# An attention and mixture-of-experts block: the maxima of two score parts in one bank, taken in one instruction

## The chip, the cores and the metric

The kernel runs on one core of a Trainium2 chip. The metric is the device time of one execution in microseconds (us). Before the change the median of three runs is 1061.35 us (1058.91 to 1062.14). The five engines of the core run side by side: PE multiplies matrices (its weight loads are shown as PEld), DVE works on vectors, ACT applies functions, POOL does general work and issues some transfers, SP issues most transfers. PE writes its products into PSUM, which has eight banks; DVE and ACT read them there.

## The reference

The input is four batches of 1024 tokens with 256 features. Layer norm with a modulation, causal attention with 16 heads of 16 features, an output projection with a gate, a second layer norm, a router that picks two of eight experts for each token, the experts (256 to 512 to 256) and a gated sum:

```python
scores = jnp.einsum('bhqd,bhkd->bhqk', Q, K) / np.sqrt(D_HEAD)
causal = jnp.triu(jnp.full((t, t), -jnp.inf, dtype=scores.dtype), k=1)
attn = jax.nn.softmax(scores + causal, axis=-1)
O = jnp.einsum('bhqk,bhkd->bhqd', attn, V)
```

The softmax needs, for each query and head, the maximum of the scores over the keys that are not later than the query. Everything is in float32.

## The kernel before

Attention works in **units**: a unit is four heads of one batch (NQD = 4 units for each of 4 batches, 16 in all, numbered u from 0 to 15). The four heads of a unit stand in the four groups of 32 partitions of `qTs[u % 3]` and `kTs[u % 3]`, so PE multiplies for four heads side by side, each in 32 of its 128 rows. Each unit needs two things. First the **maxima** of the scores, with queries in partitions and keys along the free axis: `m_parts` (line 829) fills a bank `ps_max` of 128 x 512 for one head, and `maxima` (lines 849 and 851) takes the largest of each row on DVE. These maxima are turned by PE (`max_rows`, line 861), copied by ACT and sent by SP into a spare row of `qTs`, so that they are subtracted when, second, the **scores** are multiplied again with keys in partitions: `s_parts` (line 896) fills a bank `ps_s`, `weigh` (line 913) adds the causal mask by a small bf16 product of `qmask` and `unit` (the identity), `exponential` (line 921) runs on ACT into `pt`, and `av_step` (line 940) multiplies `pt` with the values.

Both are cut into nine **steps**, so that each bank of 512 columns is full. Step i of the maxima takes the parts of `m_steps[i]`, each of them (tile of 128 queries, half of the keys, first column). Tiles 0 to 3 are the first half of the queries, tiles 4 to 7 the second; the second half needs all of the first 512 keys as well (`mf`, no mask) and then its own half (`mx`, masked in its last 128 columns). Three steps have two parts in one bank: step 1 (tile 2 with 384 columns and tile 0 with 128), step 2 (tiles 1 and 5, 256 each) and step 8 (tile 6 with 384, tile 4 with 128). The others have one part of 512.

`maxima` treats each part by itself. Where there is no mask (`mf`) it is one plain reduction (line 849). Where there is one it is a custom instruction (line 851) that adds the mask `cmask` and reduces, starting from the maximum of the unmasked half where there is one; a second, short instruction then reads the accumulator out into `mx`. So a bank with two parts takes four instructions.

`both` runs step i of the scores of unit u together with step i of the maxima of unit u + 1, in two half steps. A half step fills two score banks and two maxima banks, their matmuls in turn, then the maxima go to DVE, then the masks and exponentials of the scores; after the first half the av matmuls of the step before follow. In the first half the masks are written in four pieces of 32 columns of the array (`w = HW`), as the av matmuls that follow are; in the second half in one piece. Pool `ps_sc` has seven banks, used in turn by these four and by the small products between the steps (`ps_mi`: projections of the next batch, layer norm turns, routing of the batch before); the eighth holds `av`. A bank is free again when ACT or DVE has read it, and PE, which executes in order, waits for that. So do the other engines wait in order: what stands behind a waiting instruction waits as well.

In the main loop units 0 to 14 run `both` for all nine steps (unit 0 begins a little differently: its own maxima are taken by `m_alone`, which lets PE add the masks, lines 878 and 849), and unit 15 has scores alone. Between the steps the loop issues pieces of other work: layer norm (L67 makes the normalized rows that PE turns in line 76), projections (773, 748), the output projection (1003), the router of the batch before (240 to 331, on DVE above all, from unit 7 on), gates. A scheduler orders the instructions of each engine by its own estimates, so that the order around the steps is near the program's but not the same. Attention ends at about 753 us; then the experts run in blocks of 256 tokens (lines 550 to 567).

## Time and profile before

| | |
|---|---|
| median of three runs | 1061.35 us (1058.91 to 1062.14) |
| the profiled execution's own time | 1067.35 us |
| its span, first to last instruction | 1065.6 us |
| mean granted PE clock (1 is full speed) | 0.971 |
| instructions | 22453 |
| stretch of units 4 to 14 | 232.28 to 724.38 us: PE busy 485.67 of 492.10, DVE 385.70, ACT 265.38, clock 0.98 |
| unit 15 and the end of attention | 724.38 to 753.00 us |
| experts | 753.00 to 1065.60 us: PE busy 284.24 of 312.60 |

Busy time is the time in which an engine has an instruction under way. For PE this is not the same as useful work: matmuls overlap and their ends are modelled, so a matmul can seem busy while the next one waits. What tells is the time from the start of one piece of work to the start of the next, the idle time and what ended it, and the clock that the chip granted PE in the stretch. In the profile's groups the parts of a line are: line, engine, operation, names (out <- in) and shapes, count, busy us and mean ns of one, and the idle time of the engine just before them with what ended it.

### The profile page before, as it was taken

Reading aid. Unit: us, or ns where it says so; the run is one execution under the profiler, and the core shown is the slowest. Engines: PE = TensorE matmul, PEld = TensorE weight load, DVE = VectorE, ACT = ScalarE, POOL = GpSimd, SP = SyncE. Lnnn points to the kernel's source line nnn. Section 1 sums busy time; section 2 is a strip of 40 time slices with the busy share of each in tenths; the row PEclk is TensorE's granted clock in tenths of the full one; section 3 lists DMA queues with packets and bytes.
Section 4 is the critical chain, followed back from the end, with each engine's and each line's share of the span. In section 5 each row is a group of like instructions: output and inputs, shape, how many; then the busy total and the mean of one; then the engine's idle time right before and its main releaser. Section 6 shows DMA issues by size and latency. Waiting matters only on the chain. (4 is left out here: it accounts for less than half of the span.)

```text
span 1065.6 us, 22453 instructions
## 1 busy us (share of the span) xinstructions
PE 1009.5 (95%) x8154; PEld 597.5 (56%) x8154; DVE 750.8 (70%) x2349; ACT 509.7 (48%) x963; POOL 239.5 (22%) x231
## 2 busy tenths in 40 slices
PE   5899999999999999999999999998689999999994
PEld 4554534544544544454463444533368888888893
DVE  4787867766787877788868788782466686566761
ACT  4125654655555555655545546446313264444540
POOL 4000010000000001222001330015131764444344
PEclk9899999999999999999999999999889999999997
DMA  8310120110111202123010331002489956443432
GB/s 272 82 31 8 38 47 14 35 39 14 38 46 49 56 24 48 45 65 86 19 42 28 78 83 36 22 28 72 135 260 289 314 105 158 72 66 65 66 62 25
DMA packets 68686, 81.58 MB, mean 77 GB/s; under 512 B 19480, under 2 KB 50072, under 8 KB 68448
## 3 DMA queue, kind: packets, MB, share of 16 engines
q1 hardware_dynamic: 55008, 63.26, 21.7%
q0 software_dynamic: 13296, 16.89, 8.9%
q8 instruction: 64, 1.05, 0.4%
q14 instruction: 46, 0.38, 0.1%
q10 hardware_dynamic: 272, 0.00, 0.0%
HBM read 45.11 MB, written 24.93 MB: 66 GB/s over the span
## 5 line engine op out<-in xcount | busy, mean ns | idle before, releaser
L921 ACT ACTIVATE pt<-ps_s 128x512 f32<-128x512 f32 x576 | 313.0, 596 | 295.0 <-PE ps_s L913 183.2
L829 PE MATMUL ps_max<-kT,qT 32*128 32x512 f32 (+3 forms) x1536 | 376.6, 531 | 4.6 <-DVE mf L849 2.9
L896 PE MATMUL ps_s<-qT,kT 32*128 32x512 f32 (+3 forms) x1536 | 343.9, 527 | 4.2 <-DMA qT<-rows 2.4
L896 PEld LDWEIGHTS ps_s<-qT,kT 32*128 32x128 f32 x1536 | 134.5, 186 | 143.3 <-issue 44.9
L849 DVE TENSOR_REDUCE mf<-ps_max 128x1 f32<-128x512 f32 x256 | 164.0, 682 | 60.4 <-PE ps_max L829 55.2
L851 DVE CUSTOM_DVE_ANT_0 unused<-ps_max,cmask,mf 128x256 f32<-128x256 f32 (+3 forms) x256 | 140.5, 549 | 46.9 <-PE ps_max L829 27.1
L829 PEld LDWEIGHTS ps_max<-kT,qT 32*128 32x128 f32 x1536 | 153.4, 188 | 34.3 <-DVE mx L851 11.0
L940 PE MATMUL av<-pt,vaug 128*32 128x512 f32 (+3 forms) x1536 | 160.3, 505 | 0.8 <-ACT ot L948 0.8
L972 POOL TENSOR_TENSOR oc<-oc,rec 64x512 f32<-64x512 f32 x32 | 40.6, 1270 | 506.9 <-DMA rec<-inv 453.8
L567 POOL DMA_INDIRECT out_dram<-y,xb x67 | 107.8, 1609 | 131.1 <-DVE gs L529 55.7
L851 DVE CUSTOM_DVE_ANT_0 unused<-ps_max,cmask 128x128 f32<-128x128 f32 (+2 forms) x232 | 114.3, 493 | 29.5 <-PE ps_max L829 15.1
L550 PE MATMUL ps_h<-xt,wa 128*128 128x256 f32 (+1 forms) x608 | 125.2, 358 | 1.3 <-DVE xt L538 1.3
L561 PE MATMUL ps_y<-wb,hs 128*128 128x256 f32 x536 | 122.7, 379 | 0.0
L550 PEld LDWEIGHTS ps_h<-xt,wa 128*128 128x128 f32 x608 | 103.6, 193 | 12.3 <-DVE xt L538 1.6
L561 PEld LDWEIGHTS ps_y<-wb,hs 128*128 128x128 f32 x536 | 100.6, 190 | 13.2 <-ACT hs L554 0.2
L529 DVE SCALAR_TENSOR_TENSOR gs<-x,share,gs 128x256 f32<-128x256 f32 x201 | 85.2, 477 | 1.0
L554 ACT ACTIVATE hs<-ps_h 128x512 f32<-128x512 f32 x67 | 39.8, 597 | 86.4 <-PE ps_h L550 76.9
L940 PEld LDWEIGHTS av<-pt,vaug 128*32 128x32 f32 x1536 | 38.1, 112 | 76.4 <-issue 67.4
L343 POOL DMA_INDIRECT slots<-hr,sloti x64 | 63.7, 995 | 76.5 <-ACT sloti L342 55.5
L566 DVE TENSOR_TENSOR y<-ps_y,gs 128x256 f32<-128x256 f32 x67 | 25.9, 419 | 72.2 <-PE ps_y L561 69.6
L913 PEld LDWEIGHTS <-qmask 128*32 128x32 bf16 (+1 forms) x1328 | 30.2, 97 | 66.6 <-issue 59.1
L913 PE MATMUL ps_s<-unit,qmask 128*32 128x128 bf16 (+1 forms) x1328 | 57.5, 227 | 0.1
(220 smaller groups left out, 924.2 us busy)
## 6 DMA issues: line engine op xcount, KB each, us to landing
w_s<-in_w_dram SPq DMA_DIRECT2D x16, 512.0 KB
xb<-slots SPq DMA_DIRECT2D x29, 259.0 KB
qT<-qc SPq DMA_DIRECT2D x64, 64.0 KB
kT<-kc SPq DMA_DIRECT2D x64, 64.0 KB
oc<-ot SPq DMA_DIRECT2D x128, 32.0 KB
rec<-inv SPq DMA_DIRECT2D x32, 128.0 KB
out_dram<-x SPq DMA_DIRECT2D x8, 512.0 KB
wa<-in_w_dram SPq DMA_DIRECT2D x8, 512.0 KB
```

The costliest lines, as they stand in the source:

```text
L343: sent = nc.gpsimd.indirect_dma_start(out=slots, out_offset=bass.IndirectOffsetOnAxis(ap=at, axis=0), in_=hr[:, t, :], in_offset=None,).ins
L529: nc.vector.scalar_tensor_tensor(gs[:, j, :], gb[:, b, :], share[:, j, b : b + 1], gs[:, j, :], ALU.mult, ALU.add)
L550: nc.tensor.matmul(ps[:, k, :], w[:, dc, fc * P : (fc + 1) * P], xt[:, dc, :], start=(dc == 0), stop=(dc == NDC - 1),)
L561: nc.tensor.matmul(ps[:, j, :], hs[:, fc, j * P : (j + 1) * P], w[:, fc, :], start=(fc == 0), stop=(fc == NFC - 1),)
L567: added = nc.gpsimd.indirect_dma_start(out=out_rows, out_offset=bass.IndirectOffsetOnAxis(ap=xb[:, j, D : D + 1].bitcast(I32), axis=0), in ...
L829: nc.tensor.matmul(ps[:, at : at + n], qTs[u % 3][r : r + HW, qt * P : (qt + 1) * P], kTs[u % 3][r : r + HW, kb * 512 : kb * 512 + n], sta ...
L849: nc.vector.tensor_reduce(top, ps[:, at : at + n], AX.X, ALU.max)
L851: nc.vector.tensor_tensor_reduce(out=unused[:, 0:n], in0=ps[:, at : at + n], in1=cmask[:, 512 - n : 512], scale=1.0, scalar=st["mf", u][:, ...
L896: nc.tensor.matmul(ps[:, at : at + n], kTs[u % 3][r : r + HW, kt * P : (kt + 1) * P], qTs[u % 3][r : r + HW, (qb + 1) * 512 - n : (qb + 1) ...
L913: nc.tensor.matmul(ps[k : k + w, at : at + P], qmask[:, k : k + w], unit, start=False, stop=at == masked[-1],)
L921: nc.scalar.activation(pt[:, 0:n], ps[:, 0:n], AF.Exp)
L940: nc.tensor.matmul(av[HW * j : HW * (j + 1), 512 - n : 512], vaug[b % 2][:, kt, 4 * qd + j, :], pts[j][:, at : at + n], start=(kt == 0), s ...
```

## The change

For the maxima of units 5 to 15, in the three steps with two parts, PE adds the masks to `ps_max` as it does for the scores, and one plain reduction of the whole bank takes all maxima by pieces: in step 2 two pieces of 256 columns (the maxima of tiles 1 and 5), in steps 1 and 8 four pieces of 128 columns, of which three belong to one tile and the fourth to the other. The pieces go to a small tile `mp`; `join`, five small DVE operations in a unit, puts them together after steps 2 and 8, with the maxima of the unmasked half where there are any. For these units the parts of steps 0 and 3 are exchanged: tile 3 (masked) comes in step 0 and the unmasked part of tile 5 in step 3. For the maxima of units 0 to 4 nothing changes.

```diff
+        m_joint = [m_steps[3], *m_steps[1:3], m_steps[0], *m_steps[4:]]
+
+        def joint(u):
+            return u > NQD
+
+        def m_list(u):
+            return m_joint if joint(u) else m_steps
...
+        def tops_of(u):
+            if ("mx", u, 0) not in st:
+                both_halves = mxp.tile([P, 2, 4, 4], F32, tag="mx2", name="mx2")
+                for half in range(2):
+                    st["mx", u, half] = both_halves[:, half]
+                    st["mp", u, half] = mxp.tile([P, 4, 4], F32, tag=f"mp{half}", name="mp")
+                st["mx2", u] = both_halves
+
+        def joint_maxima(u, i, j, ps):
+
+            tops_of(u)
+            if m_size(*m_joint[i][0][:2]) == 256:
+                out, n = st["mx2", u][:, :, j, 1], 256
+            else:
+                out, n = st["mp", u, m_joint[i][0][0] // 4][:, j, :], P
+            nc.vector.tensor_reduce(out, ps.rearrange("p (a n) -> p a n", n=n), AX.X, ALU.max)
+
+        def join(u, half):
+
+            mx, mp = st["mx", u, half], st.pop(("mp", u, half))
+            nc.vector.tensor_reduce(mx[:, :, 2], mp[:, :, 0:3], AX.X, ALU.max)
+            if half == 0:
+                nc.vector.tensor_copy(mx[:, :, 0], mp[:, :, 3])
+            else:
+                mf = st["mf", u]
+                nc.vector.tensor_tensor(mx[:, :, 0], mp[:, :, 3], mf[:, :, 0], ALU.max)
+                nc.vector.tensor_tensor(mx[:, :, 1:3], mx[:, :, 1:3], mf[:, :, 1:3], ALU.max)
...
         def both(u, i, u_max, i_max):
 
             pts = []
+            two = joint(u_max) and len(m_joint[i_max]) > 1
             for h in range(2):
                 scores, tops, parts = [], [], []
                 for j in (2 * h, 2 * h + 1):
-                    for of, banks in ((s_parts(u, i, j), scores), (m_parts(u_max, i_max, (j + 2) % 4), tops)):
+                    for of, banks in ((s_parts(u, i, j), scores), (m_parts(u_max, i_max, (j + 2) % 4, two), tops)):
...
                 in_turn(*parts)
+                if two:
+                    w = P if h else HW
+                    for ps in tops:
+                        for part in m_joint[i_max]:
+                            at = part[2] + m_size(*part[:2]) - P
+                            for k in range(0, P, w):
+                                nc.tensor.matmul(
+                                    ps[k : k + w, at : at + P], unit[:, k : k + w], qmask,
+                                    start=False, stop=part == m_joint[i_max][-1],
+                                )
                 for k in range(2):
-                    maxima(u_max, i_max, (2 * h + k + 2) % 4, tops[k])
+                    (joint_maxima if two else maxima)(u_max, i_max, (2 * h + k + 2) % 4, tops[k])
                 pts.extend(weigh(i, scores, h == 0))
...
+            if joint(u_max) and i_max in (2, 8):
+                join(u_max, i_max // 8)
```

`m_parts` and `maxima` take their parts from `m_list(u)` instead of `m_steps`. The step i of unit u carries the maxima of unit u + 1, so the new instructions stand in steps 1, 2 and 8 of units 4 to 14.

More of the change, by code (lines that the diff above doesn't have):

```diff
@@ L826, in fill @@
             def fill(k):
-                qt, kb, at = m_steps[i][k]
+                qt, kb, at = m_list(u)[i][k]
                 n = m_size(qt, kb)
@@ L831, in fill @@
                     kTs[u % 3][r : r + HW, kb * 512 : kb * 512 + n],
-                    start=(k == 0), stop=(k == len(m_steps[i]) - 1 and not open_end),
+                    start=(k == 0), stop=(k == len(m_list(u)[i]) - 1 and not open_end),
                 )
-            return ps, [lambda k=k: fill(k) for k in range(len(m_steps[i]))]
+            return ps, [lambda k=k: fill(k) for k in range(len(m_list(u)[i]))]
         def maxima(u, i, j, ps, masked=()):
-            for part in sorted(m_steps[i], key=lambda part: (part in masked, part[2]), reverse=True):
+            for part in sorted(m_list(u)[i], key=lambda part: (part in masked, part[2]), reverse=True):
                 qt, kb, at = part
@@ L844, in maxima @@
                 kind = ("mx", u, half) if kb == half else ("mf", u)
+                if joint(u) and kind[0] == "mx":
+                    tops_of(u)
                 if kind not in st:
@@ L855, in maxima @@
                     )
+        def tops_of(u):
[6 more added lines that the diff above has]
+        def joint_maxima(u, i, j, ps):
+            tops_of(u)
+            if m_size(*m_joint[i][0][:2]) == 256:
[12 more added lines that the diff above has]
+                nc.vector.tensor_tensor(mx[:, :, 1:3], mx[:, :, 1:3], mf[:, :, 1:3], ALU.max)
         def max_rows(u, half):
```

## The prediction

> **What bounds the kernel now.** I read the page's busy shares first, then the loop of score steps (232 to 724 us holds all changed work) by windows, then one clean step in order of time, then the groups by shape for the prices.
>
> ```profile
> PE 1009.5 (95%) x8154; PEld 597.5 (56%) x8154; DVE 750.8 (70%) x2349; ACT 509.7 (48%) x963; POOL 239.5 (22%) x231
> ```
>
> PE is busy nearly all the time, but matmuls are pipelined, so the share does not say whether PE works or waits with one in flight. The windows do. Columns: stretch, length, busy time (instructions) of PE, PEld, DVE, ACT, POOL, granted clock, DMA.
>
> ```profile
> 282.99:297.29 14.30, 14.30 (x169) 8.33 (x168) 11.43 (x45) 8.07 (x17) 0.00 (x0) 1.00 0.08 20
> 237.19:255.70 18.51, 17.51 (x170) 8.82 (x170) 12.44 (x49) 10.44 (x20) 0.00 (x0) 0.91 0.05 10
> 414.58:432.42 17.84, 17.42 (x170) 8.91 (x169) 11.69 (x46) 10.71 (x23) 2.89 (x3) 0.90 0.13 39
> 596.30:609.06 12.76, 12.76 (x128) 5.54 (x127) 10.10 (x38) 7.42 (x18) 5.08 (x6) 1.00 0.18 55
> 641.17:656.28 15.11, 14.33 (x126) 5.92 (x125) 11.77 (x45) 9.02 (x16) 1.27 (x1) 0.89 0.16 46
> 687.65:704.43 16.78, 15.80 (x129) 6.18 (x127) 12.89 (x50) 7.33 (x15) 0.20 (x1) 0.90 0.05 10
> ```
>
> The stretches run from the first score matmul of a step to that of another. The first three are steps 1 to 3 of units 5, 4 and 8, with about as many PE instructions each; the last three are steps 2 to 4 of units 12, 13 and 14. Like work takes 14.30 in one place and 18.51 in another; 12.76 and 16.78. The long ones have PE idle and a lower clock. So there are two regimes: steps where PE works without a gap, and a few where it waits for DVE. A clean step 8 in order of time:
>
> ```profile
> 451.09 0.41 PE L913 MATMUL ps_s<-unit,qmask 128*32 128x128 bf16 x16
> 451.32 1.03 PE L940 MATMUL av<-pt,vaug 128*32 128x512 f32 x8
> ...
> 453.37 0.40 PE L913 MATMUL ps_s<-unit,qmask 128*128 128x128 bf16 x4
> 453.60 1.08 PE L773 MATMUL ps_mi<-hT,wk_s 128*128 128x256 f32 x4
> ```
>
> Sixteen narrow masks, or four full ones, hold PE for 0.23 us until the next work starts (451.09 to 451.32, 453.37 to 453.60). Every start follows the one before without a gap. A late stretch, unit 13, steps 2 and 3, shows the other regime:
>
> ```profile
> 647.68 1.12 PE L829 MATMUL ps_max<-kT,qT 32*128 32x512 f32 x2 [0.78 <-DVE mx L851]
> ```
>
> ```profile
> 645.33:648.75 3.42, 2.64 (x15) 0.94 (x13) 2.85 (x11) 2.46 (x5) 0.00 (x0) 1.00 0.00 0
> 648.75:652.16 3.41, 3.41 (x20) 1.41 (x22) 1.67 (x5) 0.83 (x2) 0.00 (x0) 0.50 0.02 2
> ```
>
> PE stands still until the maxima of step 2 free a bank, and the next 3.41 us run at clock 0.50. Seven banks are used in turn and a half step takes four, so PE can run ahead of DVE by less than a half step.
>
> **The change, part by part.** Steps 1, 2 and 8 of the eleven units 4 to 14 change (maxima of units 5 to 15): 33 steps.
>
> *Masks on PE.* Added per step: 16 narrow and 4 full bf16 matmuls with their weight loads, ahead of the score masks of the same tiling, so no change of tiling is added. By the rows above 0.23 + 0.23 = 0.46 us, and a doubled run agrees: 32 narrow masks at 728.83 us are followed by other work at 729.28, 0.45 against 0.23. I take 0.45: 33 x 0.45 = **14.9 us**, all on the path in the first regime. Bounds: 0 where PE waits anyway (counted below as gain), and 33 x 0.81 = 26.7 if each run cost its whole 0.41 and 0.40. I take the nearer row, time to the next start. PE's own work can't shrink, so no gain is possible here. The exponentials (L921) come as late as PE's following work does, so they add nothing.
>
> *Maxima on DVE.* Groups of the loop, mean ns before the last bar:
>
> ```profile
> L849 DVE TENSOR_REDUCE mf<-ps_max 128x1 f32<-128x512 f32 x176 | 113.1, 682 | 37.0 <-PE ps_max L829 32.9 <-issue 1.6 <-PE ps_mi L861 1.4
> ...
> L851 DVE DVE_READ_ACCUMULATOR2_ANT mx<- 128x1 f32 x352 | 29.2, 83 | 0.0
> L851 DVE CUSTOM_DVE_ANT_0 unused<-ps_max,cmask,mf 128x384 f32<-128x384 f32 x44 | 27.2, 618 | 1.5
> L851 DVE CUSTOM_DVE_ANT_0 unused<-ps_max,cmask 128x384 f32<-128x384 f32 x44 | 24.5, 557 | 1.5
> ...
> L851 DVE CUSTOM_DVE_ANT_0 unused<-ps_max,cmask,mf 128x128 f32<-128x128 f32 x45 | 15.7, 349 | 7.7 <-PE ps_max L829 3.0
> L851 DVE CUSTOM_DVE_ANT_0 unused<-ps_max,cmask 128x128 f32<-128x128 f32 x44 | 12.8, 292 | 13.7 <-PE ps_max L829 10.4
> ```
>
> Removed per unit, four heads each: step 1, 4 x (557 + 292 + 2 x 83) = 4.06 us; step 2 (the 256-wide groups are 483 and 424) 4.29; step 8, 4 x (618 + 349 + 166) = 4.53; together 12.9. Added: 12 reductions of 512 columns to 2 or 4 results. No row has that shape; the nearest are 682 (one result, same bank source) and L285, 512 columns to 64 results, at 678; the upper end is two reductions, 547 for 384 columns plus 277 for 128, 0.82. I take 0.68: 8.2 us. The five joining operations are near L317 (128x8, median 166 ns, 117 to 737): 0.8. DVE thus loses 3.9 us a unit, 43 in all (24 at the upper end). It starts about 0.2 us later, since it now waits for the masks; behind that wait stand the other maxima and whatever routing work follows on DVE, and PE waits for them through the banks. But a pair of heads then takes 1.4 instead of 2.0 to 2.3, so banks come free earlier against PE. The joined maxima are read by PE (L861) about a step later, which covers the joining. SP's and POOL's queues keep their work.
>
> *Steps 0 and 3 exchanged.* Step 0 gets four custom maxima (689 + 83) for four reductions (682), +0.36 us of DVE, step 3 the reverse. It matters where step 0 is already full on DVE (units 6 and 10, 12, 13): I take +0.5, between 0 and 1.4.
>
> *What DVE's relief returns.* Only waits of PE count. Against their clean twins the stretches lose 18.51 - 14.30 = 4.2 (unit 4), 3.5 (unit 8), 15.11 - 12.76 = 2.4 (unit 13), 4.0 (unit 14). Unit 8's twin is unit 9, also 14.30. Step 8 of unit 12 takes 6.80, the clean one 4.60 and 1.0 for one more small product (453.60 to the next step at 454.61): 1.2. Steps 3 and 4 of unit 11 take 9.61, those of unit 6 8.63: 1.0. Step 8 of units 5, 9 and 10 takes 4.93 for 4.60: 1.0 in all. For the rest of units 12 and 13 I put 1.0, an estimate of the same kind. Sum 18.3. In units 4 and 8 the wait is for the normalized rows (L67), which DVE makes between maxima of step 1; the masks put the second half's maxima 0.5 us later, so about 60% returns (2.6 + 2.1; PE's new order also keeps the av matmuls of four heads together there). In 13 and 14 DVE is ahead by two steps' savings, some 3 us, and the waits of 0.4 to 1.5 us go, the half clock mostly too: 2.0 + 3.5. Of the others 3.8. Together **-14.0**; bounds -4 and -22. What is late next is PE itself.
>
> The clock term rests on the rows of 645 to 652 us: PE busy 2.64 of 3.42, and the next 3.41 still halved. [...]
>
> **Sum.** 14.9 + 0.5 - 14.0 = +1.4. On the profiled execution's own 1067.35 us (span 1065.6 and 1.75 around it) this makes 1068.75; on the median of the runs shown, 6.0 us below it, 1062.7. The work behind the loop (753 to 1065 us) is untouched and starts when attention ends, so the shift passes on. A difference under 0.3%, 3.2 us, can't be told from none: the bounds are 1058.2 and 1064.5.
>
> **Rivals.** *Slower: PE's masks are paid and DVE's waits stay.* In the clean steps PE has no gap, so 0.45 is lost each time; if units 4 and 8 still wait for the rows and the halved windows stay, only some 5 us return: 14.9 + 0.5 - 5 = +10.4, 1071.8. It decides once less than 12.2 returns. For it: units 5 to 10 show clock 1.00 and no PE idle. *Faster: DVE's backlog was the root of more.* All 18.3 return and further halved windows of 3.41 us (five between 245 and 704 us, each 1.7 lost) go: some 22, 1061.35 + 15.4 - 22 = 1054.8. It decides above 18.6. For it: DVE 11 to 13 us busy of those stretches. *The change doesn't do what it says:* reducing by pieces costs as much as two reductions; DVE saves 24, about 9 returns, +6.4, 1067.8; part of the slower case.
>
> **Numbers.** No change 0.38 (likeliest, its own range 1058 to 1065), slower 0.33 (the piecewise case in it), faster 0.29. The range 1054 to 1072 reaches to both rivals' values.
>
> **What would show it.** Right: the new masks start to next start 0.22 more in each half; the piecewise reduction at 0.68; clean steps 1, 2 and 8 (units 5 to 10) 0.45 longer; steps 1 to 3 of unit 4 near 17, steps 2 to 4 of unit 14 near 14. Wrong: clean steps not longer, reductions near 0.82, halved windows as many as before, or the gains in units that have no waits now.

## The result and the profile after

The changed kernel takes 1073.21 us (median; 1070.84 to 1078.41) beside 1061.74 us of the kernel before on the same chip: ratio 1.0107, 95% interval 1.0066 to 1.0147, or 11.5 us slower. The profiled execution's own time is 1078.41 us (span 1076.7), 11.06 above that of before. The prediction said no change, 1062.7 us, with 1054 to 1072 as its range.

The page's busy shares first:

```profile
PE 1017.7 (95%) x8814; PEld 608.3 (56%) x8814; DVE 725.7 (67%) x2008; ACT 509.3 (47%) x963; POOL 239.9 (22%) x231
```

DVE has 341 instructions and 25 us less, PE 660 matmuls more. Now the six stretches that the prediction showed, each again from the first score matmul of its first step (columns: stretch, length, busy time of PE, PEld, DVE, ACT, POOL, granted clock, DMA):

```profile
280.92:296.37 15.45, 15.45 (x210) 9.27 (x209) 10.66 (x23) 8.06 (x17) 0.00 (x0) 1.00 0.08 20
236.25:253.85 17.60, 17.60 (x209) 9.82 (x209) 11.42 (x28) 10.28 (x20) 0.00 (x0) 1.00 0.05 10
419.15:436.85 17.70, 17.70 (x210) 9.91 (x209) 10.33 (x24) 10.62 (x23) 2.88 (x3) 1.00 0.13 40
605.37:617.76 12.39, 12.39 (x148) 5.56 (x146) 8.73 (x19) 7.42 (x19) 5.32 (x6) 1.00 0.19 58
648.78:665.72 16.94, 15.32 (x147) 6.47 (x146) 11.19 (x28) 9.07 (x16) 1.27 (x1) 0.80 0.14 41
698.12:712.29 14.17, 13.25 (x150) 6.06 (x148) 11.46 (x30) 7.44 (x15) 0.21 (x1) 1.00 0.06 12
```

The reader is to see four things. The clean stretch (unit 5, first row) is 1.15 us longer, 0.70 of it in step 1 and 0.45 in step 2: the masks are paid (the 0.25 beyond them stays open; (5,4), step 4 of unit 5, is 0.26 shorter). In units 4 and 8 (rows two and three) the clock is back at 1.00 and PE no longer idles, and yet they are only 0.9 and 0.1 us shorter. Unit 13 (row five) is 1.8 us *longer*, at clock 0.80: a gain had been expected there. Unit 14 (last row) did come down as forecast, to 14.17.

Where the wait of unit 4 went, in step (4,1) (step 1 of unit 4) and what follows it, before, from 237.20 us:

```profile
242.01 0.83 PE L940 MATMUL av<-pt,vaug 128*32 128x384 f32 x2
243.16 0.30 PE L76 MATMUL ps_mi<-ident,xna 128*128 128x128 f32 x1 [0.31 <-DVE xna L67]
```

And after, from 236.25 us:

```profile
241.76 1.80 PE L979 MATMUL av<-pt,vaug 128*32 128x384 f32 x16
243.49 0.33 PE L76 MATMUL ps_mi<-ident,xna 128*128 128x128 f32 x1
```

The first of the normalized rows (L67) begins 5.4 us after the step's start before, at 242.60, and 6.4 us after it in the changed kernel, at 242.63: the row comes no sooner, but sixteen av products now stand ahead of the product that needs it. Step 1 is 1.3 us longer, steps 3 and 4 are 0.7 and 0.6 shorter.

The price of the masks, in a step 8 of unit 8 in order of time:

```profile
455.52 0.41 PE L1143 MATMUL ps_max<-qmask,unit 128*32 128x128 bf16 x16
455.75 0.40 PE L952 MATMUL ps_s<-unit,qmask 128*32 128x128 bf16 x16
455.98 1.03 PE L979 MATMUL av<-pt,vaug 128*32 128x512 f32 x8
...
458.02 0.40 PE L1143 MATMUL ps_max<-qmask,unit 128*128 128x128 bf16 x4
458.25 0.39 PE L952 MATMUL ps_s<-unit,qmask 128*128 128x128 bf16 x4
458.48 1.08 PE L773 MATMUL ps_mi<-hT,wk_s 128*128 128x256 f32 x4
```

Each new group (L1143) holds PE for 0.23 us before the next starts (455.52 to 455.75, 458.02 to 458.25), as the rows of before had it: 0.46 us a step. The new DVE work, by shape, over units 4 to 14:

```profile
L883 DVE TENSOR_REDUCE mp<-ps_max 128x4 f32<-128x512 f32 x87 | 56.0, 684 | 39.8 <-PE ps_max L1143 38.1 <-PE ps_s L935 0.9 <-issue 0.7
...
L883 DVE TENSOR_REDUCE mx<-ps_max 128x2 f32<-128x512 f32 x44 | 28.3, 687 | 19.5 <-PE ps_max L1143 19.5
...
L888 DVE TENSOR_REDUCE mx<-mp 128x4 f32<-128x12 f32 x21 | 3.4, 162 | 0.3
```

The joint reduction costs 684 to 687 ns, as much as a plain one, and it mostly waits for PE (39.8 us of idle time before it, 38.1 of them ended by L1143). So both prices of the prediction hold (the joint reduction at 0.68, the masks at 0.46 where PE has no gap), and its sum does not.

**A way to read the rest.** Where the clock is halved, a stretch takes longer without more work in it: four score products of 512 columns, a head each, side by side, took 0.54 us at clock 1.00 (366.75 to 367.29, changed kernel) and 1.02 at 0.50 (649.74 to 650.76, kernel before). So each stretch is split: *work* is its length times its mean granted clock, *clock loss* is the remainder, 1.7 us for each halved window (3.41 us at 0.50, as 245.98 to 249.39 of the kernel before). This needs the trace alone. Several traces were taken of both kernels (the runs are told below); units 4 to 14 then read

| units 4 to 14, us | work | clock loss |
|---|---|---|
| before, four traces | 483.6, 481.2, 483.3, 482.9; mean 482.8 | 8.5, 10.2, 5.1, 8.5; mean 8.1 |
| after, three traces | 489.1, 490.4, 488.4; mean 489.3 | 15.4, 8.5, 13.7; mean 12.5 |
| difference | **+6.5** | **+4.4** |

In the same terms the prediction was +5.4 of work (14.9 + 0.5 - 10) and -4 of clock loss: some 4 of its 14.0 were halved clock, by the author's estimate.

Three and four traces are few for the clock. Every recorded execution also has its span and mean clock, so the whole program can be split in the same way, without telling units apart (mean, and plus or minus one standard error of the difference):

| whole program, same chip, us | executions | work | clock loss |
|---|---|---|---|
| before | 22 | 1032.3 | 28.6 |
| after | 6 | 1040.4 | 30.7 |
| difference | | **+8.1** (0.8) | **+2.1** (1.3) |

An execution of before at 1075.73 us, over 1.5% above its fastest, is left out. The work is clear. Of the clock loss the executions say only that the forecast fall of 4 did not come; the first two traced executions of the changed kernel had 2 and 3.5 us more of it than the means of their groups, so +4.4 is at the high end.

### The profile page after: what moved, and what is told of

Read it like the earlier page. It is cut to its first block, busy times and chain, and to the rows that moved or that the text cites. A ratio compares the mean times of both kernels' runs of the same rounds, so it can differ in the third digit from the quotient of the medians.

```text
span 1076.7 us, 23314 instructions
## 1 busy us (share of the span) xinstructions
PE 1017.7 (95%) x8814; PEld 608.3 (56%) x8814; DVE 725.7 (67%) x2008; ACT 509.3 (47%) x963; POOL 239.9 (22%) x231
## 5 line engine op out<-in xcount | busy, mean ns | idle before, releaser
L838 PE MATMUL ps_max<-kT,qT 32*128 32x512 f32 (+3 forms) x1536 | 371.9, 533 | 8.0 <-DVE mf L860 4.1
L838 PEld LDWEIGHTS ps_max<-kT,qT 32*128 32x128 f32 x1536 | 150.6, 187 | 35.6 <-issue 6.8
L550 PEld LDWEIGHTS ps_h<-xt,wa 128*128 128x128 f32 x608 | 104.3, 194 | 14.4 <-DVE xt L538 3.5
L862 DVE CUSTOM_DVE_ANT_0 unused<-ps_max,cmask,mf 128x512 f32<-128x512 f32 (+2 forms) x124 | 76.7, 619 | 25.3 <-PE ps_max L838 16.0
L883 DVE TENSOR_REDUCE mp<-ps_max 128x4 f32<-128x512 f32 x88 | 56.5, 684 | 39.8 <-PE ps_max L1143 38.1
L862 DVE CUSTOM_DVE_ANT_0 unused<-ps_max,cmask 128x512 f32<-128x512 f32 (+2 forms) x100 | 58.3, 583 | 20.7 <-PE ps_max L838 13.4
L952 PEld LDWEIGHTS <-qmask 128*32 128x32 bf16 (+1 forms) x1328 | 32.6, 97 | 53.1 <-issue 50.9
```

The costliest lines, as they stand in the source:

```text
L550: nc.tensor.matmul(ps[:, k, :], w[:, dc, fc * P : (fc + 1) * P], xt[:, dc, :], start=(dc == 0), stop=(dc == NDC - 1),)
L838: nc.tensor.matmul(ps[:, at : at + n], qTs[u % 3][r : r + HW, qt * P : (qt + 1) * P], kTs[u % 3][r : r + HW, kb * 512 : kb * 512 + n], sta ...
L862: nc.vector.tensor_tensor_reduce(out=unused[:, 0:n], in0=ps[:, at : at + n], in1=cmask[:, 512 - n : 512], scale=1.0, scalar=st["mf", u][:, ...
L883: nc.vector.tensor_reduce(out, ps.rearrange("p (a n) -> p a n", n=n), AX.X, ALU.max)
```

## The experiments

### Masks alone, reductions alone

Masks alone keeps the masks (L1143) and takes the maxima as before:

```diff
         def m_list(u):
-            return m_joint if joint(u) else m_steps
+            return m_steps
...
-                    (joint_maxima if two else maxima)(u_max, i_max, (2 * h + k + 2) % 4, tops[k])
+                    maxima(u_max, i_max, (2 * h + k + 2) % 4, tops[k])
...
-            if joint(u_max) and i_max in (2, 8):
-                join(u_max, i_max // 8)
```

> The 660 mask products stay on PE in the same 33 steps, but each maximum is taken as before the change, one instruction for each part (the mask is then added twice, which changes no maximum), and steps 0 and 3 are not exchanged. Theory A (masks paid in full, DVE's relief mostly lost): 33 x 0.45 = 14.9 us above the kernel before, and DVE is late by another 0.2 us per half step where PE waits for it, so 1076 to 1079 us. Rival B (most masks stand in time in which PE would wait anyway, and the loss comes from the new maxima and their order on DVE): at most half of it, below 1069. Rival C (the loss is where the halved clock windows happen to fall): no fixed price, and the difference follows the time at half clock in the two traces rather than the number of masks.

Reductions alone leaves out the mask products:

```diff
-                if two:
-                    w = P if h else HW
...
-                nc.scalar.copy(rows, ps)
+                nc.scalar.activation(rows, ps, AF.Copy, scale=0.5 if joint(u) else 1.0)
```

> The change without its masks on PE: the joint reductions, the joining and the exchange of steps 0 and 3 stay, and the maxima of units 5 to 15 then include keys that are later than the query; half of that maximum is subtracted instead of the maximum, which leaves the softmax as it is. This measures what DVE's relief returns by itself. Theory A: the changed kernel less 14.9, that is 1057 to 1060 us, some 2 to 5 us below the kernel before, far less than the 14.0 - 0.5 that the prediction returned (which would be 1048). Rival B: no faster than before or slower, 1062 to 1068, because the new order of DVE costs by itself. Rival C: anything between 1055 and 1066, with the difference in the halved windows.

Ratios are against the kernel before on the same chip, whose median was 1066.01 us here (1063.18 and 1068.17 in later groups); they are not the quotients of the medians, which are 1.0127 and 0.9914 here. Measured: masks alone 1079.55 us, ratio 1.0100 (1.0063 to 1.0137); reductions alone 1056.88 us, ratio 0.9894 (0.9858 to 0.9930). Units 4 to 14 as one window, masks alone and then reductions alone:

```profile
231.36:737.14 505.78, 499.22 (x5210) 245.05 (x5208) 385.70 (x1216) 264.87 (x540) 68.28 (x72) 0.98 0.18 44
```

```profile
229.76:710.63 480.87, 477.14 (x4551) 226.28 (x4549) 360.66 (x878) 265.12 (x540) 68.38 (x71) 0.99 0.19 46
```

DVE's busy time is 385.70 with the old maxima and 360.66 with the joint ones. By work: masks alone 497.2 (+14.4 on the mean of before), reductions alone 477.5 (-5.3). By clock loss: 8.5 and 3.4, against 8.1 before. The traces are of the slowest of six executions and of the fastest of seven; over all executions the whole program has +16.5 of work and -4.5 of clock loss with masks alone, -5.7 and -5.7 with reductions alone. What follows: the masks are paid nearly in full, so rival B falls, and the reductions do bring something by themselves. Together the two are a little *better* than their sum in work (14.4 - 5.3 = +9.1 against +6.5 by the traces, +10.8 against +8.1 by the executions), and worse in clock loss: each alone has less than the kernel before by the executions, both together do not. What separates the change from the sum of its parts is in the clock; most of what it costs is in the work.

### The order on DVE

In the changed kernel steps (11,2), (13,2) and (14,2) (unit, step) became longer than masks can explain: 6.86 us for 4.64, 5.94 to 7.13 for 4.33, 6.23 for 5.33. DVE in step 2 of unit 13, which begins at 648.78 us in the changed kernel:

```profile
648.25 0.68 DVE L883 TENSOR_REDUCE mp<-ps_max 128x4 f32<-128x512 f32 x1
...
650.15 0.42 DVE L44 BATCH_NORM_STATS2 stb<-x 128x6 f32<-128x256 f32 x1
...
652.47 0.48 DVE L240 SCALAR_TENSOR_TENSOR hr<-x,mvb,md 128x256 f32<-128x256 f32 x1 [0.30 <-issue]
652.87 1.28 DVE L883 TENSOR_REDUCE mx<-ps_max 128x2 f32<-128x512 f32 x2
```

And in the kernel before, where the step begins at 641.17:

```profile
643.02 0.17 DVE L49 TENSOR_SCALAR veb<-mvb 128x8 f32<-128x8 f32 x1
643.11 0.48 DVE L851 CUSTOM_DVE_ANT_0 unused<-ps_max,cmask,mf 128x256 f32<-128x256 f32 x1
...
645.28 0.17 DVE L57 TENSOR_TENSOR rsb<-rsb,nwb 128x8 f32<-128x8 f32 x1
645.75 0.48 DVE L240 SCALAR_TENSOR_TENSOR hr<-x,mvb,md 128x256 f32<-128x256 f32 x1 [0.30 <-issue]
```

Between the last reduction of step 1 (648.25) and the first of step 2 (652.87) stand the end of the router's layer norm (L44 to L57) and its first row (L240). Before the change only L44 to L49 stood ahead of step 2's first maximum; L51 to L56 stood among the maxima of the first pair of heads, L57 and L240 behind them. Step 2's first reduction begins 4.1 us after the step, where the first maximum began 1.9 after it. In the run of reductions alone it begins 1.6 us after the step, with L49 ahead of it and L51 to L57 behind it, and (13,2) takes 3.71 us. So the long order comes with the masks, for which the reductions wait; that the scheduler chooses it because of that wait fits, but is not shown. Two runs put this work behind the reductions:

```diff
+                last = st.pop("last", None)
+                with tc.issue_after(last) if last is not None else ExitStack():
                     if gates:
                         gates.popleft()()
```

where `last` is the step's last joint reduction; the first run does it after every changed step, the second only after step 2 of units 11, 13 and 14.

> The changed kernel with one thing added: what a loop pass issues to DVE after steps 1, 2 and 8 of units 4 to 14 (routing, layer norm, evictions of small products) is queued behind the joint reductions of that step, so it can't be put ahead of them. Theory A says that in units 11, 13 and 14 this work stood ahead of the reductions of step 2 and that PE paid for it in steps (11,2), (13,2) and (14,2), which were 2.2, 2.8 and 0.9 us longer than before: 4 to 6 us return, 1067 to 1069 us, unless the delayed work is then late for PE's small products. If that order is no cause: 1073, within 2 us.

> As the pinned kernel, but only after step 2 of units 11, 13 and 14, where the first trace of the changed kernel shows routing work ahead of step 2's joint reductions. The pinned kernel got (11,2), (13,2) and (14,2) down from 6.86, 7.13 and 6.23 to 5.05, 4.46 and 4.67 us but lost as much in (6,4), (10,4), (12,0) to (12,8), where the delayed work was late. Theory (the new order on DVE costs in these three places and nowhere else): 4 to 6 us of work below the changed kernel, 1067 to 1070 us. Rival (the delayed routing work is late for something else here too, so that a wait only moves): 1072 to 1075.

Measured: everywhere 1077.01 us, ratio 1.0091 (1.0056 to 1.0127); in three places 1068.25 us, ratio 1.0059 (1.0035 to 1.0082), where the changed kernel on the same chip has 1.0102. DVE in the same step of the second run, which begins at 645.92:

```profile
647.84 1.26 DVE L883 TENSOR_REDUCE mx<-ps_max 128x2 f32<-128x512 f32 x2
649.94 1.29 DVE L883 TENSOR_REDUCE mx<-ps_max 128x2 f32<-128x512 f32 x2 [0.84 <-PE ps_max L1143]
651.15 0.16 DVE L49 TENSOR_SCALAR veb<-mvb 128x8 f32<-128x8 f32 x1
```

The first pair is reduced 1.9 us after the step's start instead of 4.1, and steps (11,2), (13,2), (14,2) take 5.05, 4.24 and 4.67 us. Work in units 4 to 14 is 486.2, 3.1 below the changed kernel; clock loss 8.5. Done everywhere it gains the same three steps and loses (6,4), (10,4), (12,0), (12,2) and (12,8) again, 2.4, 2.1, 0.9, 0.9 and 1.3 us: there the delayed work is late in its turn, and work rises to 497.2. So the new order is a real part of the loss, some 4 us of the 11 (0.0043 of 1063 us is 4.6). The second run met its expectation in time; in work it had wanted 4 to 6 us.

### Five units alone

```diff
         def joint(u):
-            return u > NQD
+            return u in (5, 9, 13, 14, 15)
```

> The change for the maxima of units 5, 9, 13, 14 and 15 alone, whose steps 1, 2 and 8 lie in units 4, 8, 12, 13 and 14, where PE waited for DVE in the trace before; the six clean units between them keep the maxima of before. Theory A: 15 steps x 0.45 = 6.8 us of masks instead of 14.9, and all of what was returned in those units stays: 8.1 us below the changed kernel, about 1065 us, and down to 1060 if the clean units also lost by their order. If the price is rather per instruction on DVE or per exchange and not in the masks of the clean steps: 5/11 of the loss, 1067. If relief is worth what the prediction took (14.0 less the 1.5 of the clean units): 1056.

Measured 1074.49 us, ratio 1.0069 (1.0045 to 1.0094), 7.3 us above the kernel before: theory A misses by 4, and the price by number of units (5/11 of the loss) is nearest. Work is 486.0, +3.2 for 6.8 us of masks, and the clock loss is 11.9. Unit 12, which gained 1.3 us of work in the changed kernel with its masks paid (against the mean of before), has 1.3 us more here, though the maxima in its steps are joint: its gain depended on what was changed in the units ahead of it too. What the change does in a unit is not bought by changing that unit alone.

### Without the exchange of steps 0 and 3

```diff
-        m_joint = [m_steps[3], *m_steps[1:3], m_steps[0], *m_steps[4:]]
+        m_joint = m_steps
```

> The changed kernel without the exchange of steps 0 and 3. The prediction put the exchange at +0.5 us (0 to 1.4). If so: within 1 us of the changed kernel in work (span times clock 1038 to 1044), step 0 of units 6 and 10 shorter by 0.2 to 0.4 us and step 3 of the same units the same length. If the exchange is a hidden part of the loss: 3 us or more below the changed kernel in work, with the difference in steps 0 and 3.

One execution, 1070.33 us. Work in units 4 to 14 is 487.9, 1.4 below the mean of the changed kernel, which is the upper bound of the prediction (0 to 1.4). But no step 0 or 3 of these units differs by more than 0.02 us from the changed kernel's second trace, steps 0 of units 6 and 10 included, which were to become shorter; 1.7 us stand in unit 14 alone, most of it in step 7. The exchange is a small part at most, and its own price may be nothing.

### The changed kernel and the kernel before again

The first trace of the changed kernel had nine halved windows in units 4 to 14 where the kernel before had five. Is that the kernel or the execution?

> The changed kernel once more, for a second trace and more executions. Theory D, formed after the masks-only run, the run without masks and the pinned run: the profile's step times split into work (length times granted clock) and time lost to halved windows; masks add 14.9 us of work, DVE's relief takes 7 to 10 of work away, and the rest of the loss (6.8 us of the first profile) is halved clock, which depends on where the 3.41-us windows of the clock happen to cut the program. Then span times mean clock of each execution is again 1038 to 1044 (6 to 8 above the kernel before on the same chip), and the halved windows of the new trace lie partly in other steps: where (7,0), (7,3) and (11,1) aren't halved they take 6.26, 6.47 and about 7.9 us instead of 7.84, 8.12 and 9.51. If the halved windows belong to the change itself, they are in the same steps again, about 30 us of them in units 4 to 14, and every execution shows a mean clock near 0.969.

> The kernel before, one more trace. In units 4 to 14 its one trace has 483.6 us of work (length times granted clock) and 8.5 us lost to halved windows, five of them: (4,2), (8,2), (13,3), (13,7), (14,4). If the halved windows belong to the kernel's own waits, they are in the same steps again and the loss is 8 to 9 us. If their place is a matter of where the 3.41-us windows cut the program, the loss lies anywhere from 3 to 14 us and (7,0), (7,3) or (11,1), which the traces of the changed kernel have, show up here too.

> The same as the look before it, for another cut of the windows: work 482 to 485 us in units 4 to 14 by either reading; the loss 8 to 9 us in the same five steps, or 3 to 14 us in others.

> The same again: work 482 to 485 us; the loss 8 to 9 us in the same five steps, or 3 to 14 us in others. Over the four traces of the kernel before, the mean loss is set against that of the changed kernel (15.4 and 8.5 us so far).

> The changed kernel, a third trace: work in units 4 to 14 again 489 to 491 us. If the change itself brings halved windows, (7,0), (11,1) and (14,5) are halved again, as in both traces so far, and the loss is 8 us or more; if they are a matter of the cut, it may be as low as 3 us.

Measured: the changed kernel 1073.24 us, ratio 1.0102 (1.0073 to 1.0132), and 1073.81 in the third trace's execution; the kernel before 1064.97, 1064.70 and 1061.78. The table above has the sums. Theory D, that the place of the halved windows is chance, falls: the steps of one kernel agree between its traces mostly to 0.05 us, the halved windows of (4,2), (8,2) and (7,0) included. Those of units 13 and 14 vary, and (7,3) is halved in the first trace of the changed kernel alone. Lengths, with the clock where it is below 1:

| step | before, four traces | after, three traces |
|---|---|---|
| (4,2) | 7.54 to 7.55 (0.77) | 6.08, 6.09, 6.08 |
| (8,2) | 7.54 to 7.55 (0.77) | 6.09 each |
| (7,0) | 6.26 each | 7.84, 7.89, 7.88 (0.78) |
| (11,1) | 7.42 or 7.43 | 9.51 (0.82), 11.03, 11.07 (0.69) |
| (13,7) | 7.68 (0.78), 6.15, 6.15, 6.15 | 7.73, 7.76 (0.78), 9.31 (0.63) |
| (14,5) | 6.39, 9.42 (0.65), 6.38, 9.56 (0.64) | 8.87 (0.70), 7.98, 7.91 (0.79) |

So the halved windows of units 4 and 8 are gone after the change, as predicted, and others are there in units 7 and 11, which had no wait to end.

### The halved clock in units 7 and 11

In (7,0), (7,3), (11,1) and (13,7) PE makes the router's logits (L259): two products of 8 columns, then two score products of one head each, then fourteen products of 8 columns in a row, each with its own weight load. In (10,7) and (14,0) all sixteen stand in a row. In the traces of both kernels every recorded stretch of one granted clock (24 before, 22 after) begins on one grid of 3.41 us, and the shortest are 3.41 us long; a window here is one cell of it. Here is (7,0) in the kernel before, the run of products and then the two windows that it touches (length, busy, clock as above):

```profile
364.84 1.73 PE L259 MATMUL ps_mi<-gw,h2T 128*128 128x8 f32 x14
```

```profile
362.03:365.45 3.42, 3.42 (x25) 2.49 (x22) 3.10 (x11) 1.99 (x4) 0.00 (x0) 1.00 0.56 95
365.45:368.86 3.41, 3.41 (x45) 2.03 (x48) 1.94 (x5) 0.95 (x2) 0.00 (x0) 1.00 0.16 29
```

And in the changed kernel:

```profile
364.04 1.12 PE L935 MATMUL ps_s<-qT,kT 32*128 32x512 f32 x2
365.09 1.73 PE L259 MATMUL ps_mi<-gw,h2T 128*128 128x8 f32 x14
```

```profile
364.20:367.61 3.41, 3.41 (x22) 2.07 (x22) 1.68 (x5) 0.41 (x1) 0.00 (x0) 1.00 0.39 69
367.61:371.02 3.41, 3.41 (x32) 1.28 (x32) 1.40 (x4) 1.67 (x3) 0.00 (x0) 0.50 0.00 0
```

The work is the same, and PE's busy time is full in all four windows. But in the kernel before the run is cut by the end of a window (0.61 us of it lie in the first, 1.12 in the second); in the changed kernel it lies whole in the first, and the second runs at 0.50. The fifteen traces with the logits undivided hold 60 such runs of fourteen in units 4 to 14, four each. In 25 the run begins 0.02 to 2.09 us into a window: the next window is halved 25 times (in the first trace of each kernel: 0.15 before, 0.34, 0.90 and 1.24 after). In 35 it begins at 2.45 to 3.40: the next is halved in none, twice the one after it (in the same two traces: 2.77, 2.81 and 2.83 before, 3.39 after). In the four traces of the kernel before, the runs of (7,0), (7,3) and (11,1) begin at 2.67 to 3.02, all twelve just cut; in the three of the changed kernel those of (7,0) begin at 0.55 to 0.90 and those of (11,1) at 0.34 to 1.92. The grid itself lies at the same place against the first score product of the loop, 2.8 to 3.4 us of 3.41, in all twenty traces of this study (3.08 and 3.36 in the first trace of each kernel), and the steps repeat with it. So 1.2 us more in units 4 to 6 (+0.7, +0.9 and +1.3 of work, less 1.7 of clock loss) move the run of (7,0) from the end of a window to an early place in one, and there it takes 7.84 to 7.89 us instead of 6.26.

Place alone does not sort all of them, though. Behind attention, in the kernel before, a run of fourteen (1.62 us) begins 0.98 us into a window, at 810.15 us, and the next window (812.58 to 816.00) is at 1.00; in the changed kernel one begins 1.69 us into a window, at 816.44, and the next (818.16 to 821.58) is at 1.00 too. And in units 4 to 14 the same traces hold thirty runs of *sixteen* products, 1.85 us each; fourteen of them lie whole in a window, and none is followed by a halved one. This is (14,0) of the changed kernel, the run and the two windows:

```profile
692.21 1.85 PE L259 MATMUL ps_mi<-gw,h2T 128*128 128x8 f32 x16
```

```profile
691.87:695.28 3.41, 3.41 (x55) 2.93 (x55) 2.55 (x7) 1.21 (x3) 0.00 (x0) 1.00 0.15 31
695.28:698.70 3.42, 3.42 (x74) 1.91 (x62) 2.34 (x5) 1.61 (x4) 0.00 (x0) 1.00 0.07 17
```

The rest of the window differs too. Beside the fourteen of (7,0) stand two score products of one head each, which hold PE for 1.05 us (364.04 to 365.09) with 32 of its 128 rows; beside the sixteen four heads multiply side by side, four products of 384 columns in 0.43 us (693.99 to 694.42). This can be put in a number, an estimate from the rows: each product's part of the array (rows times columns, the first two numbers of its shape, over 128 x 128), times its columns at the pace of the rows (0.84 ns for a column in f32, since 256-column products of L773 start 0.216 us apart; 0.43 in bf16, since 128-column masks of L1143 start 0.056 apart), as a share of the window. Units 4 to 14 of the twenty traces have 2773 windows at full clock. With a share under 0.35 the next was halved in all 56; with 0.39 or more in none of 2682; between these in 14 of 35. In the first trace of each kernel, 278 of these windows, it is 9 of 9, none of 264 and 2 of 5. The window of (7,0) above has 0.24 in the changed kernel and 0.51 before, that of (14,0) 0.38, that of (10,7), whose sixteen lie whole in it too, 0.44, the two behind attention 0.51 and 0.52. So in these traces the windows ahead of a halved one are those with a low share; thin products, a head alone and waiting all occur in them. No run changed this share by itself: it sorts the recorded windows of this kernel, and is not shown as the cause.

Two runs were to move unit 7 against the grid: three masks in the kernel before (`return u == 6` for the masks alone), and five more groups of mask products in the changed kernel.

```diff
-                    for ps in tops:
+                    twice = (u_max, i_max) in ((6, 1), (6, 2), (6, 8), (7, 1), (7, 2))
+                    for n, ps in [(n, ps) for n in range(1 + twice) for ps in tops]:
```

> The kernel before with the mask products on PE in three steps alone, steps 1, 2 and 8 of unit 5 (the masks are added twice there, which changes no maximum). Theory H, from fourteen traces: the 3.41-us windows of the clock stand at the same place against the first score product of the loop each time (2.8 to 3.4 us), so what moves work within the loop decides which windows are halved. In four traces of the kernel before the 14 logits products of (7,0) begin 2.70 to 3.00 us into a window, are cut by its end and nothing is halved; in the changed kernel they begin at 0.55 to 0.90, lie whole in one window, and the next is halved each time. Three masks of 0.45 move them by 1.35 us to 0.6 to 0.95: (7,0) is halved and takes 7.8 us instead of 6.26; (7,3) is moved by 1.35 + 1.6 to 2.2 to 2.6 and is not halved, 6.47. Together 3.0 us for three masks. If the halving has nothing to do with place: (7,0) 6.26 us, and 1.35 in all.

> The changed kernel with the mask products of five steps issued twice, steps 1, 2 and 8 of unit 5 and steps 1 and 2 of unit 6 (the first pass adds zeros), 5 x 0.45 = 2.25 us more on PE ahead of unit 7. Theory H: the 14 logits products of (7,0) begin at 2.8 to 3.15 us into a window instead of 0.55 to 0.90 and are cut: (7,0) is not halved and takes 6.26 us instead of 7.84, though PE has more to do; (7,3) then begins at 0.1 to 0.9 and is halved, 8.1 us. If the masks bring the halved window by themselves, (7,0) stays at 7.84.

Both missed, in their premise. Three masks moved the run by 0.39 us, not 1.35: steps 1 and 2 took 0.45 longer (5.72 to 6.17, 4.60 to 5.05), but (5,4) and (6,0) became 0.2 and 0.3 shorter, and (5,8) only 0.11 longer: the likely reason, not shown, is that later work on PE ends a wait for DVE as well as faster work on DVE does. The run began at 3.13, was cut, and (7,0) took 6.26. In the other run (1085.27 us) the five groups cost 0.46 each, but units 0 to 3 took 0.8 us longer than in two of the three traces, and the grid lay 0.2 to 0.5 us earlier, so that the run of products came round a whole window to 0.59: (7,0) was halved again. Both agree with the sorting by place, and neither was the test of it that it should have been. What is said of the clock here rests on the recorded windows, not on a run that switched one.

### The logits in two parts

```diff
-        def logits(half):
+        def logits(half, k):
             ps = misc()
-            for i in range(4):
+            for i in (2 * k, 2 * k + 1):
...
-            (row, 6, logits, 0), (row, 7), (turned, 1, 0), (turned, 1, 1), (logits, 1), (compare,),
+            (row, 6, logits, 0, 0), (row, 7, logits, 0, 1), (turned, 1, 0), (turned, 1, 1), (logits, 1, 0),
+            (logits, 1, 1, compare),
```

> The changed kernel with the router's logits issued in eight products of 8 columns each instead of sixteen at a time, in neighbouring steps, for a test of what halves the clock. In the traces so far a window in which the sixteen products lie together (PE busy without a gap, but 8 columns for each weight load) is followed by a halved one when it holds most of them, at (7,0), (7,3), (11,1) and (13,7). Theory D: these halvings go whatever the phase, two to four windows of 3.41 us, so 3 to 6 us less time at half clock (mean clock 0.974 or more against 0.969 to 0.971) and 1068 to 1071 us; the work is the same or up to 1 us more. If only PE's idle time halves the clock: the same clock and 1073 us or, for the two more evictions, 1074.

> The changed kernel with both repairs: routing work queued behind step 2's reductions in units 11, 13 and 14 (alone: 4.3 us below the changed kernel) and the router's logits issued eight at a time (alone: 4.7 below). Theory E: the change lost what the prediction had returned in these two places, the new order on DVE and the halved windows behind the router's sixteen small products; they are separate, so both together give 8 to 9 us, 1.5 to 3 us above the kernel before, near the +1.4 that the prediction summed. Rival F: they are the same loss seen twice (the halved windows follow the waits): 5 us together, 6 above the kernel before.

> The kernel before the change with the logits issued eight at a time: the control for the split. If the change brought the halved windows behind the logits (theory E), the split gives the kernel before little, 0 to 2 us (its trace has one such window, at (13,7)). If the kernel before loses as much there on the mean of its executions (rival G), the split gives it 4 to 5 us as well, and the logits are no part of why the change lost.

> The kernel without masks (joint reductions alone; maxima of units 5 to 15 include later keys, half of them is subtracted) with both repairs. Theory E: without masks step (11,2) alone had the new order's wait (6.12 for 4.64 us), so 1 to 3 us below the run without masks: 13 to 14 us below the kernel before. The difference between the changed kernel with both repairs and this one is then the masks alone: 14.9, against the 21 to 22 us between them without repairs. Rival F: 11 below the kernel before, and 17 or more between the two.

> The masks alone (maxima taken as before, the mask added twice) with the logits issued eight at a time, to complete the table of masks and joint reductions. Theory E: the masks cost 14.9 us over the kernel before with the same split, less the 1 to 3 us that stand where PE would wait: 12 to 14 above it. Rival G: the split gives the masks-only kernel as much as any other, 4 to 5 us, so 7 to 8 above the kernel before without the split.

| logits in two parts, with | median, us | ratio to before | work, units 4 to 14 | clock loss |
|---|---|---|---|---|
| the changed kernel | 1068.55 | 1.0055 (1.0031 to 1.0079) | 490.6 | 5.1 |
| the changed kernel, three places pinned | 1068.33 | 1.0009 (0.9981 to 1.0038) | 490.0 | 5.1 |
| the kernel before | 1060.59 | 0.9930 (0.9899 to 0.9960) | 482.5 | 10.2 |
| reductions alone, three places pinned | 1048.52 | 0.9825 (0.9790 to 0.9860) | 472.3 | 5.1 |
| masks alone | 1073.74 | 1.0047 (1.0017 to 1.0076) | 496.4 | 0.0 |

In the changed kernel (7,0) falls from 7.89 to 6.16 us and (11,1) from 11.03 to 7.77, (7,3) is halved instead, and the time falls by 4.7 us: theory D's expectation in time, though not "whatever the phase". With both repairs the changed kernel can't be told from the kernel before as it stood (1.0009), as theory E had it. But that is no fair pair, since the kernel before gains 0.70% from the split too, which is rival G's outcome: with the same split it is 1060.59, 7.7 us below the changed kernel with both repairs. Its one trace shows no gain in units 4 to 14 (work 482.5, clock loss 10.2), but that is of the second slowest of twelve executions, 1066.10. Over all executions the split takes 2.6 of work and 4.4 of clock loss (1.8) from the kernel before, and 0.8 and 3.9 (1.7) from the changed one. So the split is worth having by itself, both kernels gain about as much by it, as far as these errors tell, and the logits are not shown to be what the change lost by. And masks against none, with both repairs, differ by 19.6 us (0.0184 of 1068), where theory E wanted 14.9 and rival F 17 or more; masks alone against none in the kernel before, both split, differ by 12.5 (0.0117), which is the 12 to 14 that E had.

The split of the kernel before computes what the kernel before does and beats both; reductions alone with both repairs is faster still, but it subtracts half of a maximum over too many keys, which is safe only while the scores stay moderate.

## Why the prediction was wrong

- **Masks, 14.9.** Right: 0.23 us for each group, 0.45 for a clean step ((5,2), (9,2), (10,2): 4.60 to 5.05 in every trace, though (5,1) took 0.70 and (5,8) 0.11 more); the masks alone add 14.4 of work.
- **Exchange, 0.5.** Between nothing (steps 0 and 3 the same to 0.02 us) and 1.4, in one trace; inside its bounds.
- **Reductions at 0.68, joining 0.8 a unit.** Right: 0.684 to 0.687; the joining took about 1.0 (10.7 us in eleven units). DVE's busy time fell by 24 us, not 43: the short instructions of before already overlapped (at 451.50 us one starts 0.07 before the 0.35-us maximum from 451.22 ends), and summed durations (37.5 us less) counted that overlap twice.
- **Relief returned, -14.0: this step failed.** It held some 10 of work and 4 of halved clock. With masks at 14.9 and the exchange at 0 to 1.4, the +6.5 of work in the traces mean that 8.4 to 9.8 came back, the +8.1 of all executions 6.8 to 8.2: less than 10, and by other places. The clock term was -4 and came out at +4.4 in the traces, +2.1 over all executions: 8.4 of the 9.5 us by which +1.4 missed +10.9, or 6.1 of 8.8 by the executions. So in all some 5 us returned instead of 14.0. Of the halved windows in the prediction's four long stretches those of (4,2) and (8,2) went. (13,3) kept its own in two traces of three, and unit 14's, at (14,4) or (14,5) in three traces of four before, is at (14,5) in all three. The prediction held everything else fixed, and so had no term for windows that come: (7,0), (11,1), one more in (13,7). How much of the rest of the loss is due to them, and how much to the new order on DVE (some 4 us by the pinned run), stays open, since the kernel before gains as much by dividing the logits.
- **By place.** Taking 1.35 us of masks out of each unit, the means of the traces give a return of 2.4 in unit 4 (predicted 2.6), 1.3 in unit 8 (2.1), 1.6 in unit 14 (3.5), and -1.1 in unit 13 (2.0), where the new order on DVE held step 2's banks. The other seven units returned 4.9 of work (3.8) and lost 5.1 to the clock.
- **Sentence by sentence.** "In units 4 and 8 the wait is for the normalized rows": PE's idle time there ended, at clock 1.00, but in unit 4 not because the rows came sooner: PE has the av products to do meanwhile, as the prediction's remark in brackets had it. "DVE is ahead by two steps' savings" in units 13 and 14: false in step 2 of both, since the scheduler spent the lead on routing work first. The prediction took DVE's order as it was.
- **The rivals.** The slower one, 1071.8 us, is nearest in number: it had some 5 us returned, and 5.4 were (at most 9.8 less 4.4 of clock). Its mechanism, that units 4 and 8 go on waiting and the old windows stay halved, is not what happened. Of the signs named for a right prediction the masks' 0.23, the reductions' 0.68 and unit 14's 14 us came; of those for a wrong one, "halved windows as many as before" did.

No run shows the 4 us of halved clock that the 14.0 held: they were the author's estimate, and the runs showed +4.4 and +2.1 in their place. The windows ahead of halved ones were of both kinds. In (4,2) of the kernel before PE waited, busy for 3.00 of 3.42 us (242.56 to 245.98), and the next window ran at 0.50; in (7,0) of the changed kernel PE was busy for 3.41 of 3.41 us, with a share of 0.24 of the array at work, and the next ran at 0.50 as well.

## What to carry to other kernels

Price a change in work and in halved clock apart (length times granted clock, and the rest), and take several traces and the clock of all executions: a step that repeats to 0.05 us is the kernel's own, a halved window included, but three traces don't give a mean. Relief from a wait can be real and still be spent: here by a scheduler that put routing work first (step 2 of unit 13, its first reduction 4.1 us after the step instead of 1.9) and beside halved windows that came elsewhere ((7,0): 7.84 us instead of 6.26). Read the new order of every engine before predicting, and put into the range that windows may come as well as go. Try a repair on the kernel before as well: here it gained as much. In the clean steps PE was busy without a gap, and 0.45 us a step added to it was paid (4.60 to 5.05); DVE's busy time fell by 24 us, and 8.4 to 9.8 of work came back by the traces.

## What the runs showed of the hardware

- Sixty runs of fourteen 8-column products in units 4 to 14 (1.73 us each, fifteen traces): begun up to 2.09 us into a 3.41-us window, the next window ran at half clock in 25 of 25; begun at 2.45 us or later, in 0 of 35. None began between those two. Two such runs behind attention (1.62 us), begun at 0.98 and 1.69, were followed by clock 1.00. Of thirty runs of sixteen (1.85 us each), fourteen of them whole in a window, none was followed by half clock.
- The share of the array at work (the estimate above) sorts 2773 windows of units 4 to 14 in twenty traces: under 0.35 the next was halved in 56 of 56, from 0.39 in 0 of 2682, between in 14 of 35. These are counts in variants of one kernel; what sets the clock was not shown.
- Windows in which PE waited went both ways: that of (13,2) in the changed kernel (650.92 to 654.33), 1.79 us busy of 3.41, was followed by clock 0.50, and one of 3.00 us busy of 3.42 in the kernel before (242.56 to 245.98) too; one of 2.70 us busy of 3.42 there (703.36 to 706.78) was followed by 1.00. Busy time alone does not sort them; the shares are 0.31, 0.32 and 0.35.
- A reduction of 128 x 512 from a bank took 683 ns to one result, 684 to four and 687 to two (means of units 4 to 14, changed kernel); four instructions for the same bank took 1.17 us from one bank's start to the next (step 8 at 451.22 and 452.39 us of the kernel before).
